# An audio tower on one core: scores and value products of two heads packed side by side in TensorE, a transposed group norm, and new start rounds

## Chip, cores and metric

The kernel runs on one core of a Trainium2 chip. Times are device microseconds (us) of one execution. Engines: PE is TensorE (PEld its weight loads), DVE is VectorE, ACT is ScalarE, POOL is GpSimd, SP is SyncE, which issues the DMAs.

## What is computed

The input is 32 sequences of 160,000 samples. Each is padded and cut into S = 313 frames of 512 samples. One layer of an audio tower follows (the reference, cut to what matters):

```python
h = frames @ dct.T                                   # (32, 313, 512)
X = layernorm(h)
Q, K = xpos(X W_Q), xpos(X W_K, downscale)           # 8 heads of 64
p = softmax(Q K^T) * gamma_h ** |s - t|
Y = groupnorm_per_head(p V) * gn_weight + gn_bias
h = h + (silu(X W_G) * Y) @ W_O
x = layernorm(h)
theta = x[..., None, :] / (1 + |W|) + B_param        # 256 units x 512 features
sin, cos = table(round(theta * 4096 / 2 pi) mod 4096)
h = h + silu(sum_d(cos * a_cos) @ P_cos.T + sum_d(sin * a_sin) @ P_sin.T)
```

The feature part is the large one: for each of 32 x 313 frames, 256 x 512 sines and as many cosines.

## The kernel before

The work has two kinds, which run interleaved on the same engines: **attention** of one sequence (function attention, L302), and **feature rounds** (ffn_round, from L574).

*Feature rounds.* The sequences go in 16 pairs. STARTS (L33) gives the round in which each pair enters; it stays eight rounds, one for each block of 32 of the 256 units. A round therefore works on one to four pairs, r = 2 to 8 sequences. A round has 128 (unit, 128 features) parts, taken in slots of up to 24 sequences x 313 columns. In each slot DVE computes indices, one instruction per part (L612), adds a quarter turn (L621) and masks (L628); ACT takes two sines of up to 7512 columns (L636), into one of two trig buffers; PE contracts them with a one-hot attention matrix into four-way column groups (L658). At the end of a round sums are copied (L675) and stored (L682, L688). The features of the ring come from DRAM (xT, L596), and the contraction's weights too (hot, L604).

*Attention.* A sequence uses one set of buffers, A: PSUM banks W (four), and in SBUF h (rows), u, xnT, prob (8 heads x 3 row tiles x 313). The rows are held in three tiles of N = 105 rows. In order: DCT (rows, L282), layer norm with Newton steps on POOL, transposes (L269), values (L282), rotated queries and keys for pairs of heads (columns, L297, then L360 and L363), scores, exponentials on ACT (L400), and for each head nine transposes of the probabilities (L428), the decay (L440), and the product with the values. Then the gate, the group norm, the output product, and the second layer norm, whose transposed result goes to xT_d (L525). A function output (L528) ends a pair once its eight rounds are over. The first two sequences run before any feature round, side by side, in buffers A and B; all others run in A beside the rounds. While one pair is in the ring (r = 2), attention takes its copies and row sums on ACT, otherwise on DVE.

*Steps that the change touches.* scores (L367): per head, three matmuls of 64 contracted rows x 313 columns into banks 0 to 2 (L374), then one maximum (L382) and one subtraction (L385) over 3 x 313 columns; the next head uses the same banks. Product with values (L446): for each head and row tile, three matmuls with the probabilities as weights and 64 columns of values, result in rows, copied for two heads at a time (L460). Group norm: square (L481 or L478), sum over 64 columns (L486), reciprocal and three small steps (L488 to L491), Newton on POOL, a POOL product (L495), a broadcast product (L498), twelve transposes (L269), weight and bias from PSUM (L509), product with the gate (L514).

*What sets the order.* Plan (L46) collects every step with a key, an engine, an expected duration and what it reads and writes. emit (L63) then simulates the engines and writes out, for each, the ready step with the smallest key. The keys of a feature round count sines: one unit is one full sine. attention spreads its keys over the time that it was given: step(n) adds n to a counter, and the key is that share of 135. The time for each sequence comes from STARTS: the kernel takes the tightest spacing that has each pair ready eight units before its round. What comes out is a fixed order on every engine; at run time an instruction also waits for the one ahead of it on its engine.

Of the kernel before, what the change touches and what calls it, by code (L numbers as in the profile page):

```python
# [21 lines left out]
P = 128  # L22
# [5 lines left out]
EPS = 1e-5  # L28
RING = 8
# [3 lines left out]
STARTS = (0, 4, 8, 10, 12, 14, 16, 18, 20, 22, 24, 26, 28, 30, 32, 34)  # L33
# [93 lines left out]
def tile_audio_tower(ctx: ExitStack, tc: tile.TileContext, t: dict, out: bass.AP):  # L127
# [23 lines left out]
    class Buffers:  # L151


        def __init__(self, name, pool, psum):
# [16 lines left out]
            self.h = sb("h", NT, HOP)  # L171
            self.xnT = sb("xnT", NC4, S)
# [11 lines left out]
            self.sq = wide[:, : NT * HOP].rearrange("p (i d) -> p i d", d=HOP)  # L184
            self.hres = self.sq
            self.aff = wide[:, NT * HOP : NT * HOP + NC4 * S].rearrange("p (c s) -> p c s", s=S)
            self.mx = [sb(f"mx{i}", NT) for i in range(2)]
# [7 lines left out]

            self.y = self.W[:, 3, : NT * 2 * DH].rearrange("p (i d) -> p i d", d=2 * DH)
# [24 lines left out]
    def rsqrt(plan, key, val, r, u, kv, kr, ku):  # L221
# [17 lines left out]
        plan.add(key, "POOL", 6000, newton, (kv,), (kr, ku))  # L239
# [24 lines left out]
    def transposed(plan, key, x):  # L264

        for c in range(NC4):
            def go(c=c):
                for i in range(NT):
                    nc.tensor.transpose(  # L269
                        x.W[:, c, ROW0[i] : ROW0[i] + N], x.h[:N, i, c * P : (c + 1) * P],  # L270
                        ident[:N, :N],
                    )
            plan.add(key, "PE", 800, go, x.rows_of, x.banks(c))

    def rows(plan, key, x, lhsT, src, r, order=range(NT), src_r=()):

        for c in range(NC4):
            k = x.load(plan, key, src[c], src_r)
            for to, i in enumerate(order):
                plan.add(  # L280
                    key, "PE", 880,
# [7 lines left out]
    def columns(plan, key, x, bank, src):  # L289
# [4 lines left out]
        for c in range(NC4):  # L294
            plan.add(
                key, "PE", 550,
# [5 lines left out]
    def attention(plan, keys, sq, x, eng, swap_m=None):  # L302
# [6 lines left out]
        def step(n=1.0):  # L309
            done[0] += n  # L310
            return keys(done[0] / 135.0)
# [14 lines left out]
        plan.add(step(0), "SP", DMA_NS, lambda: nc.sync.dma_start(x.u, t["frames"][sq]), (), us)  # L326
        rows(plan, step(7), x, x.u, t["dct"], us)
        copy(plan, step(), eng, NT * HOP, x.h[:N], W3, x.banks(0, 1, 2), hs)
        residual(step(0), False)
        layernorm(plan, step(3), x)  # L330
        transposed(plan, step(3), x)
        copy(plan, step(), eng, NC4 * S, x.xnT, x.W[:, :, :S], x.banks(0, 1, 2, 3), (x.k("xnT"),))


        rows(plan, step(7), x, x.xnT, wv_d, (x.k("xnT"),), range(NT - 1, -1, -1),
             ("wv_d",))
        copy(plan, step(), eng, NT * HOP, x.h[:N], W3, x.banks(0, 1, 2), hs)
        plan.add(step(0), "POOL", 500, lambda: nc.gpsimd.memset(x.h[0:1, : NT - 1, :], 0.0), (), hs)

        plan.add(step(0), "SP", DMA_NS, lambda: nc.sync.dma_start(x.table, t["turn_qk"]),  # L340
                 (), probs[-4:-2])

        def rotary(g):
            key = step(4)
# [7 lines left out]
            else:  # L352
                copy(plan, key, eng, 2 * S, x.raw, x.W[:, 0:2, :S], x.banks(0, 1), probs[-1:])
                for i in range(2):
                    plan.add(key, "PE", 550,
# [11 lines left out]
        def scores(hd):  # L367
            key = step(2.5)
            r0 = (hd % 2) * DH
            qk, kq = x.qk[hd // 2 % 2], x.k("u", hd // 2 % 2)  # L370
            for i in range(NT):
                plan.add(
                    key, "PE", 660,
                    lambda i=i: nc.tensor.matmul(  # L374
                        x.W[:N, i, :S], qk[r0 : r0 + DH, 0, ROW0[i] : ROW0[i] + N],
                        qk[r0 : r0 + DH, 1, :], start=True, stop=True,
                    ),
                    (kq,), x.banks(i),
                )
            m = x.mx[hd % 2]  # L380
            plan.add(key, "DVE", 1150,
                     lambda: nc.vector.tensor_reduce(m[:N], x.W[:N, :NT, :S], AX.X, ALU.max),  # L382
                     x.banks(0, 1, 2), (x.k("mx", hd % 2),))
            plan.add(key, "DVE", 1150,
                     lambda: nc.vector.tensor_tensor(  # L385
# [554 lines left out]
```

## Time and profile before

| what | us |
|---|---|
| median of 3 runs | 18587.15 (18586.4 to 18591.35) |
| the profiled execution's own time | 18593.15 |
| its span, first to last instruction | 18591.2 |
| ACT busy | 17827.2 |
| DVE busy | 17165.7 |
| PE busy | 14520.5 |
| POOL busy | 968.9 |

The span is 2 us shorter than the execution's own time. Busy times are of the profiled execution. In the groups a line reads: source line, engine, operation, output <- input, shapes, count | busy us, mean ns of one | idle us of the engine just before them, and what ended it. In the table of stages each row is a stretch of the span with each engine's busy us and its count of instructions, then PE's granted clock, the DMA share and GB/s. In the waits a row is the waiting engine and line, what it waited for, total us, times, longest us. An fp32 matmul leaves two records in the trace, a transpose one. A matmul's mean duration includes the time that it overlaps others, so PE's cost is taken as busy us divided by the count.

### The profile page before, as it was taken

The page shows a single profiled execution, that of the slowest core. Times are in us where ns is not written, and L with a number is a line of the kernel's source. Part 1 is how long each engine was busy: PE and PEld are TensorE (multiplying, and loading weights), DVE is VectorE, ACT ScalarE, POOL GpSimd, SP SyncE. Part 2 cuts the span into 40 slices and gives each one's busy share as a digit, 9 for nine tenths or more (in the row PEclk, how much of TensorE's full clock was granted, in tenths as well). Part 3 has the DMA queues.
Part 4 walks back from the last instruction along what each step waited for, and adds up shares of the span by engine and source line. Part 5 has one row for each costly group of instructions (what it writes and reads, how often), then busy time and mean ns, then how long its engine had stood idle before and what let it go on. Part 6 is the DMA issues. An engine that isn't in the chain of part 4 may idle for free. (4 is left out here: it accounts for less than half of the span.)

```text
span 18591.2 us, 325962 instructions
## 1 busy us (share of the span) xinstructions
PE 14520.5 (78%) x148768; PEld 6791.6 (37%) x148768; DVE 17165.7 (92%) x11210; ACT 17827.2 (96%) x3248; POOL 968.9 (5%) x1222
## 2 busy tenths in 40 slices
PE   8788888888777877778877787877788777666666
PEld 5443333334333333333333333333333333222222
DVE  6989999999999999999999999999999999888887
ACT  4899999999999999999999999999999999999998
POOL 0000000000000000000000000000000000000000
PEclk8899999999999999999999999999999999888888
DMA  3221121121111111111111111111111111001011
GB/s 94 71 66 56 60 67 58 54 61 58 45 38 47 57 50 52 45 45 57 48 58 47 43 53 48 58 48 55 39 50 57 48 56 42 29 21 33 20 40 53
DMA packets 598691, 942.55 MB, mean 51 GB/s; under 512 B 116768, under 2 KB 337952, under 8 KB 586048
## 3 DMA queue, kind: packets, MB, share of 16 engines
q1 hardware_dynamic: 597312, 921.70, 16.0%
q8 instruction: 1166, 19.10, 0.4%
q14 instruction: 213, 1.74, 0.0%
HBM read 816.78 MB, written 104.66 MB: 50 GB/s over the span
## 5 line engine op out<-in xcount | busy, mean ns | idle before, releaser
L636 ACT ACTIVATE trig<-ix 128x7512 f32<-128x7512 int16 (+1 forms) x2760 | 17398.1, 6386 | 456.8 <-PE pa L658 229.7
L658 PE MATMUL pa<-trig,hot 128*32 128x313 f32 x131072 | 10304.5, 468 | 3545.1 <-ACT trig L636 3530.3
L658 PEld LDWEIGHTS pa<-trig,hot 128*32 128x32 f32 x131072 | 4291.2, 118 | 9312.4 <-ACT trig L636 4578.4
L612 DVE TENSOR_SCALAR ix<-xT,f 128x2504 int16<-128x2504 f32 (+3 forms) x5376 | 6499.2, 1268 | 431.6 <-ACT trig L636 389.4
L628 DVE TENSOR_SCALAR ix<-ix 128x15024 int16<-128x15024 int16 (+4 forms) x1656 | 5581.8, 3385 | 41.1
L621 DVE TENSOR_SCALAR ix<-ix 128x7512 int16<-128x7512 int16 (+1 forms) x1380 | 2905.2, 2105 | 356.1 <-ACT trig L636 264.4
L297 PE MATMUL a_W<-a_xnT,a_ring 128*128 128x313 f32 x4896 | 1426.2, 437 | 40.9 <-DVE a_prob L385 15.4
L282 PE MATMUL a_W<-a_ring,a_u 128*105 128x512 f32 x2256 | 1087.5, 625 | 141.2 <-DMA a_u<-in_frames 52.9
L297 PEld LDWEIGHTS a_W<-a_xnT,a_ring 128*128 128x128 f32 x4896 | 891.8, 190 | 580.1 <-issue 212.5
L282 PEld LDWEIGHTS a_W<-a_ring,a_u 128*105 128x105 f32 x2256 | 374.7, 177 | 756.3 <-issue 615.0
L233 POOL TENSOR_TENSOR a_gu<-a_gr 105x24 f32<-105x24 f32 x93 | 104.5, 1124 | 9461.6 <-DVE a_gr L227 9456.7
L446 PE MATMUL a_W<-a_h,a_prob 105*105 105x64 f32 x4464 | 483.0, 264 | 77.6 <-DVE a_prob L440 77.4
L374 PE MATMUL a_W<-a_u 64*105 64x313 f32 x1488 | 477.7, 453 | 72.1 <-DVE a_prob L385 40.0
L446 PEld LDWEIGHTS a_W<-a_h,a_prob 105*105 105x105 f32 x4464 | 447.3, 177 | 212.1 <-issue 143.7
L282 PE MATMUL a_W<-a_ring,a_xnT 128*105 128x512 f32 x744 | 350.6, 611 | 22.3 <-DVE a_xnT L219 20.5
L233 POOL TENSOR_TENSOR a_lu<-a_lr 105x3 f32<-105x3 f32 x186 | 141.1, 759 | 4073.3 <-DVE a_lr L227 4063.6
L374 PEld LDWEIGHTS a_W<-a_u 64*105 64x105 f32 x1488 | 234.0, 171 | 310.8 <-DVE a_prob L385 79.2
L428 PE MATMUL a_W<-ident,a_prob 105*105 105x105 f32 x2232 | 284.9, 272 | 44.1 <-DVE a_h L460 26.1
L382 DVE TENSOR_REDUCE a_mx<-a_W 105x3 f32<-105x939 f32 x248 | 280.1, 1130 | 37.6 <-PE a_W L374 36.5
L428 PEld LDWEIGHTS a_W<-ident,a_prob 105*105 105x105 f32 x2232 | 237.9, 178 | 159.4 <-issue 92.5
L440 DVE TENSOR_TENSOR a_prob<-a_W,a_u 105x939 f32<-105x939 f32 x248 | 279.8, 1128 | 16.3 <-PE a_W L428 10.9
L385 DVE TENSOR_TENSOR a_prob<-a_W,a_mx 105x939 f32<-105x939 f32 x248 | 281.7, 1136 | 8.5
(134 smaller groups left out, 3386.8 us busy)
## 6 DMA issues: line engine op xcount, KB each, us to landing
hot<-in_hot SPq DMA_DIRECT2D x1344, 128.0 KB
xT<-xT_d SPq DMA_DIRECT2D x88, 1252.0 KB
a_u<-in_decay SPq DMA_DIRECT2D x248, 260.5 KB
a_ring<-in_proj SPq DMA_DIRECT2D x128, 256.0 KB
a_ring<-in_dct SPq DMA_DIRECT2D x124, 256.0 KB
a_ring<-wv_d SPq DMA_DIRECT2D x124, 256.0 KB
a_ring<-in_wq SPq DMA_DIRECT2D x124, 256.0 KB
a_ring<-in_wk SPq DMA_DIRECT2D x124, 256.0 KB
```

The source lines that it names most:

```text
L282: lambda c=c, i=i, k=k, to=to: nc.tensor.matmul(x.W[:N, to, :], lhsT[:, c, ROW0[i] : ROW0[i] + N], x.ring[k], start=(c == 0), stop=(c == N ...
L297: lambda c=c: nc.tensor.matmul(x.W[:, bank, :S], w[:, c, :], x.xnT[:, c, :], start=(c == 0), stop=(c == NC4 - 1)),
L374: lambda i=i: nc.tensor.matmul(x.W[:N, i, :S], qk[r0 : r0 + DH, 0, ROW0[i] : ROW0[i] + N], qk[r0 : r0 + DH, 1, :], start=True, stop=True,),
L382: lambda: nc.vector.tensor_reduce(m[:N], x.W[:N, :NT, :S], AX.X, ALU.max),
L385: lambda: nc.vector.tensor_tensor(x.prob[:N, hd], x.W[:N, :NT, :S], m[:N].unsqueeze(2).to_broadcast((N, NT, S)), ALU.subtract),
L428: nc.tensor.transpose(x.W[:N, jj, ROW0[i] : ROW0[i] + N], x.prob[:N, a, i, ROW0[j] : ROW0[j] + N], ident[:N, :N],)
L446: nc.tensor.matmul(x.y[:N, i, (hd % 2) * DH : (hd % 2 + 1) * DH], x.prob[:N, a, jj, ROW0[i] : ROW0[i] + N], x.h[:N, jj, hd * DH : (hd + 1) ...
L612: nc.vector.tensor_scalar(ix[:, x[0], pt * r * S : (pt + 1) * r * S], now["xT", y][:, : r * S], f[:, 0, n : n + 1], f[:, 1, n : n + 1], AL ...
L621: nc.vector.tensor_scalar(ix[:, x[1], :E], ix[:, x[0], :E], float(LUT // 4), None, ALU.add)
L628: nc.vector.tensor_scalar(ix[:, i, :E], ix[:, i, :E], LUT - 1, LUT // 2, ALU.bitwise_and, ALU.bitwise_xor)
L636: nc.scalar.activation(tl[:, :E], ix[:, x[1 - k], :E], AF.Sin, bias=-PI32, scale=ANG)
L658: nc.tensor.matmul(now["pa", p][g * 32 : g * 32 + 32, :S], now["hot", hot[n // 4 * 4, c]][:, n % 4, k, :], now["trig", w][:, s0 : s0 + S], ...
```

## The change

It has five parts.

1. *Planned durations and shares.* The key of attention's steps now follows a table of shares (SHARE, TIMES) instead of counts out of 135; several expected durations are changed. The feature matmuls' key becomes one unit smaller.
2. *Scores.* Two heads at a time: for each row tile one matmul of rows 0 to 63 and one of rows 64 to 127, into two banks; the next row tile takes the other two banks. Maximum and subtraction are taken for two heads x one row tile.
3. *Product with values.* For two heads, 3 x 2 matmuls with the values as weights (64 columns each, into PSUM rows 0 to 63 and 64 to 127) and 313 columns of probabilities. The result is transposed, two heads in one bank, and is copied so (yT). The values are kept in an order (v) that gives each pair of heads a stretch of its own, in the same buffer.
4. *Group norm in transposed form.* Square of yT; sums of each head by twelve matmuls with a 0/1 table of 8 columns; variance in two fused steps, which take the softmax's row sum in without a reciprocal; Newton as before; three transposes of the factors, a copy, four matmuls that spread them over the 512 features with gn_weight in the table; one product; bias and gate in one fused step for each of four tiles. The twelve transposes, the POOL product and the scaled copies go. Two small tables are loaded for each sequence.
5. *Start rounds.* STARTS is changed; there are 43 rounds where there were 42.

```diff
-STARTS = (0, 4, 8, 10, 12, 14, 16, 18, 20, 22, 24, 26, 28, 30, 32, 34)
+STARTS = (0, 4, 7, 9, 11, 13, 15, 17, 19, 21, 23, 25, 27, 29, 32, 35)
...
+SHARE = dict(rows=5.0, copy=2.5, norm=8.0, turn=0.7, rotary=4.2, scores=6.4, exps=2.0, head=3.5,
+             pair=0.8, gate=4.1, silu=1.5, group=7.0, affine=5.0)
...
-        def step(n=1.0):
-            done[0] += n
-            return keys(done[0] / 135.0)
+        def step(stage=None):
+
+            if stage:
+                done[0] += SHARE[stage]
+            return keys(done[0] / WHOLE)
...
+        def scores(g):
...
             for i in range(NT):
+                b = (g * NT + i) % 2 * 2
+                m, km = x.mx[(g * NT + i) % 2], x.k("mx", (g * NT + i) % 2)
+
+                def go(i=i, b=b):
+                    for a in range(2):
+                        nc.tensor.matmul(
+                            x.W[:N, b + a, :S], qk[a * DH : a * DH + DH, 0, ROW0[i] : ROW0[i] + N],
+                            qk[a * DH : a * DH + DH, 1, :], start=True, stop=True)
+                plan.add(key, "PE", 690, go, (kq,), x.banks(b, b + 1))
...
+            def go(g=hd // 2):
+                for jj in range(NT):
+                    for b in range(2):
+                        nc.tensor.matmul(
+                            x.W[b * DH : (b + 1) * DH, 3, :S],
+                            x.v[:N, jj, g, b * DH : (b + 1) * DH],
+                            x.prob[:N, 2 * g + b, jj, :], start=(jj == 0), stop=(jj == NT - 1))
+            plan.add(key, "PE", 1900, go, (*probs[hd - 1 : hd + 1], hs[hd // 2]), x.banks(3))
...
+        def sums():
+            for i in range(NT):
+                for c in range(NC4):
+                    nc.tensor.matmul(x.W[:N, 0, i * H : (i + 1) * H],
+                                     x.sqT[:, c, ROW0[i] : ROW0[i] + N], x.of_head[:, c, :],
+                                     start=(c == 0), stop=(c == NC4 - 1))
+        plan.add(key, "PE", 2400, sums, room, x.banks(0))
...
+            nc.vector.scalar_tensor_tensor(f(x.gv), f(x.sm), EPS, f(x.sm), ALU.mult, ALU.mult)
+            nc.vector.scalar_tensor_tensor(
+                f(x.gv), x.W[:N, 0, : NT * H], 1.0 / DH, f(x.gv), ALU.mult, ALU.add)
...
+        def factors():
+            for i in range(NT):
+                nc.tensor.transpose(x.W[:H, 1, ROW0[i] : ROW0[i] + N], x.gr[:N, i, :], ident[:N, :N])
...
+        def spread():
+            for c in range(NC4):
+                nc.tensor.matmul(x.W[:, c, :S], x.head_w[:, c, :], x.rT, start=True, stop=True)
...
+                     lambda: nc.vector.tensor_tensor(x.sqT, x.yT, x.W[:, :, :S], ALU.mult),
...
+                     lambda c=c: nc.vector.scalar_tensor_tensor(
+                         x.u[:, c, :], x.sqT[:, c, :], gnb[:, c : c + 1], x.u[:, c, :],
+                         ALU.add, ALU.mult),
...
-                plan.add(key, "PE", 150 * len(parts) * r, go,
+                plan.add(key - 1, "PE", 150 * len(parts) * r, go,
```

## The prediction

> **What bounds the kernel now.** I read the busy shares first, then the groups with the idle time before them, then the busy time by stage, and last who waited for whom.
>
> ```profile
> PE 14520.5 (78%) x148768; PEld 6791.6 (37%) x148768; DVE 17165.7 (92%) x11210; ACT 17827.2 (96%) x3248; POOL 968.9 (5%) x1222
> ...
> L636 ACT ACTIVATE trig<-ix 128x7512 f32<-128x7512 int16 (+1 forms) x2760 | 17398.1, 6386 | 456.8 <-PE pa L658 229.7
> L658 PE MATMUL pa<-trig,hot 128*32 128x313 f32 x131072 | 10304.5, 468 | 3545.1 <-ACT trig L636 3530.3
> ...
> L446 PE MATMUL a_W<-a_h,a_prob 105*105 105x64 f32 x4464 | 483.0, 264 | 77.6 <-DVE a_prob L440 77.4
> ...
> L374 PE MATMUL a_W<-a_u 64*105 64x313 f32 x1488 | 477.7, 453 | 72.1 <-DVE a_prob L385 40.0
> ```
>
> The sines (L636) are 17,398 of ACT's 17,827 us, and ACT's work is the same in both kernels. So the time is 17,827 us plus ACT's idle time, 18591.2 - 17827.2 = 764 us; a change can gain only from that. Where it lies, by stage (columns: start and end, length, then busy us of PE, weight load, DVE, ACT, POOL):
>
> ```profile
> 0.00:316.20 316.20, 265.07 (x992) 171.67 (x992) 144.94 (x178) 51.44 (x125) 19.96 (x82) 0.79 0.35 106
> 316.20:1003.00 686.80, 552.00 (x5104) 283.40 (x5104) 630.16 (x749) 587.07 (x201) 44.68 (x76) 0.89 0.24 72
> 1003.00:2215.00 1212.00, 985.73 (x9777) 483.37 (x9770) 1162.63 (x943) 1136.17 (x246) 69.68 (x89) 0.92 0.19 59
> 2215.00:2806.00 591.00, 481.71 (x4733) 224.76 (x4735) 569.60 (x468) 552.32 (x97) 42.91 (x63) 0.93 0.23 70
> 2806.00:4531.00 1725.00, 1413.30 (x14272) 686.80 (x14264) 1668.17 (x1128) 1663.91 (x281) 125.14 (x152) 0.94 0.18 57
> 4531.00:15750.00 11219.00, 8950.55 (x92936) 4185.94 (x92940) 10587.96 (x6210) 11079.16 (x1857) 666.55 (x760) 0.93 0.16 49
> 15750.00:18541.00 2791.00, 1845.53 (x20928) 746.51 (x20916) 2398.21 (x1536) 2754.23 (x445) 0.00 (x0) 0.88 0.10 32
> 18541.00:18591.20 50.20, 26.61 (x52) 9.17 (x48) 4.00 (x3) 2.90 (x2) 0.00 (x0) 0.77 0.34 97
> ```
>
> Length less ACT gives the idle time: **265 us** before the first sine, 100 + 76 + 39 + 61 = **275 us** in the ramp to 4531, **140 us** in the steady stage, **37 us** at the end, **47 us** after the last sine. In the first stage PE is the busy engine (265 of 316 us). In the ramp DVE is (92 to 97%). In the steady stage ACT itself is at 98.8%.
>
> ```profile
> ACT trig L636 <- PE pa L658: 229.7, 132, 8.8
> ACT trig L636 <- DVE ix L628: 128.1, 56, 13.4
> ACT trig L636 <- issue: 81.3, 21, 7.4
> ```
>
> These waits are the sines': for PE to give a trig buffer back, and for DVE to deliver indices. "issue" has no named cause; those that I followed in the timeline lay beside a held-up PE, and I count it with PE.
>
> [...] four 32-wide groups make one feature record cost 10304.5/131072 = 79 ns, against 1426.2/4896 = 291 ns for a full-width one of the same 313 columns (L297). For row halves no run shows it: L374 uses one half at a time, 477.7/1488 = 321 ns. [...] the trace's clock is 0.50 from 150 to 200 us, where the prelude does transposes and 64-column products.
>
> **The change, part by part.** An fp32 matmul leaves two records here, a transpose one.
>
> *PE, per sequence.* Removed: product of weights and values 483.0/31 = 15.6 us, scores 477.7/31 = 15.4, the gate's twelve transposes 1.7; in all 32.7. Added: 24 products of 313 columns, 48 x 291 ns = 14.0, halved when the two heads share the columns, 7.0; scores halved, 7.7; 12 sums at L446's 108 ns x 24 = 2.6; three transposes 0.4; four spreads 8 x 291 ns = 2.3. In all 20, so -12.7 us (if nothing overlaps: 34.7, +2). After the prelude PE is not the bound, so this alone counts little there.
>
> *DVE, per sequence.* Maxima and subtractions: 8 x (1130+1136) = 18.1 us become 24 x 809 = 19.4 (+1.3). Reduce, reciprocal and three small steps, 2.58, become two small ones, 0.37 (-2.2). L509 and L514, 3.85, become four of about 0.53 (-1.7). Square, product and result copies shrink with 1536 to 1252 columns and 0.55 to 0.48 us (-0.9). The copy of the factors adds 0.5. Sum **-3.0 us**. The fused operation and the one that reads PSUM are not in the trace; at 0.48 to 0.80 us each it is -3.2 to -1.9.
>
> *Starts of the pairs.* DVE's index instructions are 128 in every round however many sequences it holds; the four rows (602, 927, 1254, 1578 ns for 626 to 2504 columns) give a fixed 276 ns, so a round costs 35 us of DVE beyond its elements. The new starts have 43 rounds for 42, but reach the same point (the start of the sixth pair) in 13 rounds where it took 14. So the ramp loses 35 us of DVE work, and 70 us appear at the end, where DVE is at 86%. Sines: 2758 for 2760, no difference.
>
> *Prelude (265).* Two sequences run on PE. The heads' stage is 157.7 to 233.5 us, of blocks such as these:
>
> ```profile
> 213.38 3.38 PE L446 MATMUL a_W<-a_h,a_prob 105*105 105x64 f32 x18
> 216.56 1.86 PE L428 MATMUL b_W<-ident,b_prob 105*105 105x105 f32 x9
> ```
>
> Sixteen products at about 3.0 us are 48 us. They become eight of 12 records; [...] 2.7 us each: 22 us. That is -26 if paired, -4 if not. The scores took 47.7 us in two stretches, where PE and DVE took turns on the same banks; with alternating banks DVE alone sets them, 24 x 1.62 + 3 = 42: -5. The longer chain of the group norm (sums, factors, spread: three more PE hops and a copy) adds about 6 where PE has nothing else. **-25**, from -5 to -35.
>
> *Ramp (275).* DVE-paced, so DVE work removed comes back as time: 35 us and ten sequences by 3 us, -65. One stall is plain:
>
> ```profile
> 1005.30 1.77 DVE L612 TENSOR_SCALAR ix<-xT,f 128x1252 int16<-128x1252 f32 x2 [19.41 <-DMA xT<-xT_d]
> ```
>
> The second pair's features landed late, and ACT lost 13.4 us. In the order of the kernel as built, the last copy of that pair stood one slot (two sines) ahead of its round; it now stands 2.5 ahead, and at the later starts 2 to 9, where it was mostly 1 to 3. That is -13. The feature matmuls get a key one unit earlier, so attention goes before them only when it lags a sine; of the ramp's some 170 us of PE waits most will be overtaken by DVE, I take -17. **-95**, from -30 (only part of the DVE work) to -200 (DVE's floor is 4031 - 65 = 3966 us for 4215).
>
> *Steady (140).* 67 us of the waits here are PE's and 48 "issue". The earlier key and 12.7 us less PE work per sequence shorten the stretches for which a feature block stands behind attention; stalls in which PE waits for a transfer (L282 for in_frames, 34 us in 15 waits) stay. I take half of 115: **-60**, from 0 to -105.
>
> *End (84).* A third round of one pair costs DVE 143 us against ACT's 138, +5; the last output is as before. **+5**, from 0 to +20. The two table loads per sequence add two SP issues, each of 0.3 to 0.6 us like its neighbours, with the gate's columns to hide them; without that cover, under 1 us per sequence. The extra round brings 32 loads of hot, four of xT and four of f on SP, spread over 138 us. POOL loses one step (L495) and clears the same 1024 elements in four pieces; at 5% busy nobody waits for it.
>
> Sum -25 - 95 - 60 + 5 = **-175 us**. The profiled execution took 18593.15 us, 6 above the median of 18587.15, so against the median: **18,412 us** (-0.94%).
>
> **Rivals.** (a) *Pairs don't overlap in the array.* For it: row halves are in no trace[...]. Against: the column groups do overlap. The prelude keeps -5 and the steady stage loses a third: about 18,455. (b) *PE waits only change their name:* DVE has 94% in the steady stage and more in the ramp, so the freed sines wait for indices. Then -25, -50, -10, +5: 18,507. (c) *The stalls nearly all go*, since accurate durations let the written order fit the chip: -30, -170, -100, 0: 18,290. (d) *Slower: attention falls behind.* One buffer serves every sequence in turn; three more PE hops now stand behind feature blocks of 3.4 us each, and the spacing in the ramp shrinks from 64 to 58.7 sines (413 to 379 us). If the last copy comes later than about two slots before its round, each start costs ACT the 13.4 us seen above; at all 15 starts 201 us, more than the gain from the fourteenth start on: 18,613. Against: the order as built has the copies earlier, not later. (e) The change does what it says: the built kernel has the counts above, so this is not open.
>
> **How the numbers follow.** Main case 0.55 (18,340 to 18,470), (a) 0.12, (b) 0.18, (c) 0.10, (d) 0.05. The range 18,300 to 18,515 covers the main case, (a), (b) and part of the way to (c). About 0.2%, 37 us, is what a measurement of this kernel can tell from no change: faster needs under 18,550. From the cases: faster 0.92, same 0.05, slower 0.03.
>
> **What would show it.** First sine near 290 us for 316; 12-record products near 2.7 us in the prelude; scores' groups at about 160 ns of PE a record; DVE busy about 60 us lower (-97 + 35); ACT busy within 5 us of 17,827; PE waits of the sines near half of 230; no wait of 19 us for xT at the fifth round. It is wrong if ACT's idle time in the ramp stays above 240 us, or if the sines' waits for DVE grow by what those for PE lose.

## The result, and the profile after

The changed kernel takes **18551.99 us** (median of 20 runs, 18542.69 to 18563.74) against 18588.39 for the kernel before (20 runs): a ratio of **0.9981, with an interval from 0.9975 to 0.9987**. It is faster by 36 us where 175 were predicted, and it lies above the range. The profiled execution has a span of 18548.7 us, 42.5 less than before.

The page of the changed kernel, busy times and then the groups that the change was about (line, engine, operation, shapes, count | busy us, mean ns | idle us before them):

```profile
PE 14237.3 (77%) x146432; PEld 6376.6 (34%) x146432; DVE 17101.3 (92%) x11500; ACT 17818.3 (96%) x3246; POOL 1062.2 (6%) x1190
...
L660 ACT ACTIVATE trig<-ix 128x7512 f32<-128x7512 int16 (+1 forms) x2758 | 17391.4, 6391 | 430.3 <-PE pa L682 184.7
L682 PE MATMUL pa<-trig,hot 128*32 128x313 f32 x131072 | 10303.9, 468 | 3675.0 <-ACT trig L660 3636.7
...
L391 PE MATMUL a_W<-a_u 64*105 64x313 f32 x1488 | 267.5, 465 | 123.3 <-DVE a_mx L396 103.1
...
L466 PE MATMUL a_W<-a_prob,a_h 105*64 105x313 f32 x1488 | 235.0, 452 | 41.2 <-DVE a_prob L455 40.8
```

The work went the way that was forecast, on PE with less of it gone. The scores (L391) are 267.5/1488 = 180 ns a record for 321 before (160 forecast), the products of values and weights (L466) 235.0/1488 = 158 ns for the 291 of a full-width record, so in both the two of a pair run together. PE has 283 us less, 9 per sequence where 12.7 were forecast; DVE has 64 us less (62 forecast). The maxima and subtractions of 626 columns, forecast at 809 ns, took 801 and 809 (L396, L400); before, an operation on two tensors of that width took 811 (L363). The fused steps of 313 columns, forecast at 0.53 us, took 0.54 (L535). But the sines' idle time fell only from 456.8 to 430.3 us.

Stage by stage, as before, but cut where the same sine starts (sine 0, 610 and 2340, counted from 0, each cut within 0.3 us; columns: start and end, length, busy us of PE, weight load, DVE, ACT, POOL, then clock, DMA share and GB/s). First the kernel before, then the changed one:

```profile
0.00:316.50 316.50, 265.07 (x992) 171.67 (x992) 145.24 (x179) 51.74 (x125) 19.96 (x82) 0.79 0.35 106
316.50:4568.30 4251.80, 3465.83 (x34147) 1691.55 (x34148) 4059.62 (x3312) 3965.81 (x827) 290.49 (x392) 0.92 0.20 62
4568.30:15862.30 11294.00, 9002.35 (x93488) 4206.44 (x93486) 10648.62 (x6231) 11158.63 (x1871) 658.47 (x748) 0.93 0.16 50
15862.30:18591.20 2728.90, 1787.24 (x20144) 721.95 (x20144) 2312.18 (x1492) 2651.02 (x429) 0.00 (x0) 0.87 0.10 31
```

```profile
0.00:313.60 313.60, 227.86 (x846) 122.09 (x846) 138.31 (x190) 51.21 (x125) 17.91 (x80) 0.83 0.36 108
313.60:4534.20 4220.60, 3383.19 (x33496) 1570.55 (x33496) 4018.18 (x3228) 3975.82 (x827) 353.46 (x370) 0.92 0.21 61
4534.20:15830.50 11296.30, 8801.53 (x91692) 3928.07 (x91692) 10557.84 (x6318) 11147.77 (x1865) 669.49 (x716) 0.93 0.17 49
15830.50:18548.70 2718.20, 1824.73 (x20400) 755.91 (x20398) 2386.98 (x1766) 2643.48 (x433) 21.38 (x24) 0.89 0.13 38
```

So the difference in length is **-2.9 in the prelude, -31.2 in the ramp, +2.3 in the steady stage and -10.7 at the end**, where -25, -95, -60 and +5 were forecast. The forecast was of ACT's idle time, which is length less ACT's busy time: 264.8 and 262.4 us, 286.0 and 244.8, 135.4 and 148.5, 77.9 and 74.7, so **-2, -41, +13 and -3**. The two counts differ because the same number of sines is not the same work: some sines, those of the last slot of a round, have fewer than 7512 columns. Counted in full sines of 7512 columns, the ramp holds 599.3 before and 601.3 after, and the end 414.7 and 412.0.

The steady stage gained nothing although PE has 201 us less to do in it (9002.4 to 8801.5) and DVE 91. Its waits, of the sines and then of PE (PE's own waits for sines left out):

```profile
ACT trig L660 <- issue: 107.0, 25, 7.5
ACT trig L660 <- PE pa L682: 35.0, 19, 4.7
```

```profile
PE a_W L391 <- DVE a_mx L396: 68.7, 41, 3.4
PE a_W L517 <- POOL a_gr L247: 60.0, 18, 5.0
```

Before, those two rows of the sines had 48.5 and 62.2 us. The wait for PE was halved, as forecast, and the one without a named cause doubled. PE's second row is new: the factors' transposes (L517) stand for POOL's Newton steps. One such place in the timeline (POOL, PE, DVE and ACT mixed, weight loads left out; start us, length us, then in brackets the idle time ahead and its releaser):

```profile
9979.29 4.07 DVE L652 TENSOR_SCALAR ix<-ix 128x15024 int16<-128x15024 int16 x1
9979.44 3.99 POOL L246 TENSOR_SCALAR a_gu<-a_gu 105x24 f32<-105x24 f32 x1
9980.58 3.37 PE L682 MATMUL pa<-trig,hot 128*32 128x313 f32 x48 [1.45 <-ACT trig L660]
...
9988.07 0.21 POOL L246 TENSOR_SCALAR a_gu<-a_gu 105x24 f32<-105x24 f32 x1
9988.36 0.23 POOL L247 TENSOR_TENSOR a_gr<-a_gr,a_gu 105x24 f32<-105x24 f32 x1
9988.65 0.69 PE L517 MATMUL a_W<-ident,a_gr 105*8 105x105 f32 x3 [4.70 <-POOL a_gr L247]
9989.38 0.47 DVE L520 COPY a_prob<-a_W 8x313 f32<-8x313 f32 x1 [3.02 <-PE a_W L517]
...
9989.90 4.54 PE L524 MATMUL a_W<-a_prob 8*128 8x313 f32 x8 [0.57 <-DVE a_prob L520]
...
9994.37 8.23 PE L682 MATMUL pa<-trig,hot 128*32 128x313 f32 x96
...
9999.56 12.82 ACT L660 ACTIVATE trig<-ix 128x7512 f32<-128x7512 int16 x2 [6.33 <-issue]
```

Read it from the bottom. ACT lost 6.33 us at 9999.56. It needed a trig buffer that PE gives back with a feature block, and PE's last block had ended at 9983.95. Until 9994.37, for 10.4 us, PE did none: it stood 4.70 us for POOL, transposed, waited for a copy, and spread the factors. A feature block frees one buffer and takes 3.4 us; a sine takes 6.4. The POOL step L246 took 3.99 us here, where it lay beside DVE's L652 and ended 0.07 us after it, and 0.21 us at 9988.07. The whole Newton chain took 13.0 us here; the planner was told 7.5.

Part of the 10.4 us is a slower PE. In the table of stages, cut at this place, the granted clock stands third from the right (a block ahead of the wait, the wait, the stretch behind it, the next block):

```profile
9980.58:9983.95 3.37, 3.37 (x48) 1.46 (x48) 3.37 (x2) 3.37 (x1) 3.29 (x2) 1.00 0.00 0
9983.95:9988.65 4.70, 0.00 (x1) 0.00 (x1) 2.40 (x2) 4.70 (x2) 3.99 (x9) 0.89 0.09 28
9988.65:9994.37 5.72, 5.15 (x11) 2.70 (x12) 4.08 (x3) 4.58 (x1) 0.00 (x0) 0.50 0.01 3
9994.37:9999.56 5.19, 5.19 (x57) 2.13 (x60) 5.05 (x6) 0.00 (x0) 0.00 (x0) 0.66 0.39 121
```

The clock was 1.00 in the first 3.5 us of the stand and 0.50 from 4 us on, and 0.50 through the stretch behind it. The eight records of the spread (L524) took 4.54 us; at 4936.49 us, at a clock of 1.00, they took 2.37. ACT got its buffer 5.2 us after the block behind them began, where a block at a clock of 1.00 took 3.37 (at 9980.58). An estimate from these figures: about 4 of the 6.33 us that ACT lost came with the slower clock (4.54 - 2.37 and 5.2 - 3.37), the rest with the stretch itself. Of the 19 such places of the steady stage the spread took over 4.5 us in 13.

### The profile page after: what moved, and what is told of

It is laid out like the page before. It is cut to its first block, busy times and chain, and to the rows that moved or that the text cites. A ratio compares the mean times of both kernels' runs of the same rounds, so it can differ in the third digit from the quotient of the medians.

```text
span 18548.7 us, 322240 instructions
## 1 busy us (share of the span) xinstructions
PE 14237.3 (77%) x146432; PEld 6376.6 (34%) x146432; DVE 17101.3 (92%) x11500; ACT 17818.3 (96%) x3246; POOL 1062.2 (6%) x1190
## 5 line engine op out<-in xcount | busy, mean ns | idle before, releaser
L660 ACT ACTIVATE trig<-ix 128x7512 f32<-128x7512 int16 (+1 forms) x2758 | 17391.4, 6391 | 430.3 <-PE pa L682 184.7
L636 DVE TENSOR_SCALAR ix<-xT,f 128x2504 int16<-128x2504 f32 (+3 forms) x5504 | 6535.1, 1246 | 145.8 <-ACT trig L660 111.2
L652 DVE TENSOR_SCALAR ix<-ix 128x15024 int16<-128x15024 int16 (+4 forms) x1655 | 5582.3, 3387 | 43.0
L308 PE MATMUL a_W<-a_xnT,a_ring 128*128 128x313 f32 x4896 | 1452.9, 440 | 34.3 <-DVE a_prob L374 8.9
L244 POOL TENSOR_TENSOR a_lu<-a_lr 105x3 f32<-105x3 f32 x186 | 186.0, 1000 | 4411.5 <-DVE a_lr L238 4239.7
L400 DVE TENSOR_TENSOR a_prob<-a_W,a_mx 105x626 f32<-105x626 f32 x372 | 301.1, 809 | 76.9 <-PE a_W L391 58.8
L391 PE MATMUL a_W<-a_u 64*105 64x313 f32 x1488 | 267.5, 465 | 123.3 <-DVE a_mx L396 103.1
L396 DVE TENSOR_REDUCE a_mx<-a_W 105x2 f32<-105x626 f32 x372 | 297.9, 801 | 26.3 <-PE a_W L391 20.5
L466 PE MATMUL a_W<-a_prob,a_h 105*64 105x313 f32 x1488 | 235.0, 452 | 41.2 <-DVE a_prob L455 40.8
L374 DVE TENSOR_TENSOR a_prob<-a_W,a_prob 128x1252 f32<-128x1252 f32 x124 | 180.6, 1457 | 45.6 <-PE a_W L370 37.7
L428 DVE TENSOR_REDUCE a_sm<-a_prob 105x6 f32<-105x1878 f32 x108 | 220.0, 2100 | 0.0
```

Source lines behind the costliest of these rows:

```text
L244: nc.gpsimd.tensor_tensor(u, r, r, ALU.mult)
L308: lambda c=c: nc.tensor.matmul(x.W[:, bank, :S], w[:, c, :], x.xnT[:, c, :], start=(c == 0), stop=(c == NC4 - 1)),
L396: lambda b=b, m=m: nc.vector.tensor_reduce(m[:N], x.W[:N, b : b + 2, :S], AX.X, ALU.max),
L400: lambda i=i, b=b, m=m: nc.vector.tensor_tensor(x.prob[:N, 2 * g : 2 * g + 2, i, :], x.W[:N, b : b + 2, :S], m[:N].unsqueeze(2).to_broadca ...
L636: nc.vector.tensor_scalar(ix[:, x[0], pt * r * S : (pt + 1) * r * S], now["xT", y][:, : r * S], f[:, 0, n : n + 1], f[:, 1, n : n + 1], AL ...
L652: nc.vector.tensor_scalar(ix[:, i, :E], ix[:, i, :E], LUT - 1, LUT // 2, ALU.bitwise_and, ALU.bitwise_xor)
```

## The experiments

Theory: the steady stage's gain went into this new stretch of PE. Rivals: PE's total of attention work between blocks holds the sines whatever its order; or the earlier key or the new starts did the harm. All changes are against the changed kernel unless said otherwise. Stages are cut at the same sines, from one profiled execution each; the medians are of all runs of each kernel. The kernel before was run again beside each group of experiments, with medians from 18585.8 to 18595.1 us, and the ratios are to those; a difference of 10 us between two experiments is within that spread.

| kernel | median us | to sine 0 | to 610 | to 2340 | to the end |
|---|---|---|---|---|---|
| before | 18588.4 | 316.5 | 4251.8 | 11294.0 | 2728.9 |
| changed | 18552.0 | 313.6 | 4220.6 | 11296.3 | 2718.2 |
| 1 Newton planned at 16 us | 18474.9 | 312.8 | 4214.3 | 11229.1 | 2716.9 |
| 2 Newton on DVE | 18456.8 | 313.0 | 4218.9 | 11207.3 | 2717.1 |
| 3 key back | 18558.5 | 318.2 | 4228.2 | 11286.4 | 2711.8 |
| 4 starts back | 18574.2 | 319.9 | 4222.3 | 11320.7 | 2724.0 |
| 5 order in the prelude | 18541.1 | 310.8 | 4223.1 | 11290.7 | 2716.7 |
| 6 scores back | 18538.9 | 311.9 | 4226.6 | 11292.6 | 2717.2 |
| 7 all Newton on DVE | 18508.5 | 307.4 | 4252.9 | 11223.1 | 2720.4 |
| 8 = 2 + 5 | 18450.7 | 311.1 | 4206.4 | 11210.6 | 2717.0 |
| 9 spread one block later | 18444.9 | 318.4 | 4213.2 | 11193.4 | 2714.0 |
| 10 = 2 + 4 | 18474.0 | 314.7 | 4218.1 | 11209.8 | 2724.0 |
| 11 = 2 + 5 + 6 | 18448.0 | 306.0 | 4209.8 | 11220.8 | 2710.5 |
| 12 = 11, prelude's Newton on DVE | 18431.1 | 300.3 | 4205.2 | 11222.0 | 2714.1 |
| 13 = 9 + 5, prelude's Newton on DVE | 18438.5 | 309.1 | 4217.4 | 11203.6 | 2713.1 |
| 14 = 13 + 6 | 18413.8 | 302.0 | 4219.7 | 11177.2 | 2714.0 |
| 15 norm ahead of the gate | 18428.3 | 308.8 | 4185.1 | 11215.7 | 2713.7 |
| 16 = 14 + 15 | 18403.8 | 293.2 | 4217.2 | 11178.2 | 2708.1 |

Kernels with the same order on PE up to the first sine (the changed one, 2, 3 and 4 among them) put it anywhere from 313.0 to 319.9 us, so first sines are compared below by their pieces.

**1, a longer planned duration of Newton.**

```diff
-        plan.add(key, "POOL", 7500, newton, (kv,), (kr, ku))
+        plan.add(key, "POOL", pool, newton, (kv,), (kr, ku))
...
-        rsqrt(plan, key, x.gv[:N], x.gr[:N], x.gu[:N], x.k("gv"), x.k("gr"), x.k("gu"))
+        rsqrt(plan, key, x.gv[:N], x.gr[:N], x.gu[:N], x.k("gv"), x.k("gr"), x.k("gu"),
+              16000 if eng == "DVE" else 7500)
```

> The changed kernel (18552 us) with one number different: the planner takes 16 us, not 7.5, for POOL's Newton steps of the group norm (as they take 12.6 to 13 us in the steady stage of the trace), which puts three feature blocks instead of two between the sums and the factors' transposes on PE, and in most sequences one more block before the spread. My theory, that PE standing for POOL in those transposes (60 us in 18 waits of the steady stage) is where the steady stage lost what it was to gain: the wait falls below 10 us, the sines' idle time without a named cause (107 us in the steady stage) halves, and the time falls by 40 to 70 us, to about 18,500. Rival, that the sines are held by PE's total of attention work between blocks and the wait only changes its name: within 15 us of 18,552.

18474.89 us, ratio to before 0.9941 (0.9929 to 0.9954), 77 us below the changed kernel. The sines' wait without a cause fell to 41.3 us, but PE's wait for POOL only to 40.7. The expected size of the gain was right and its reason only half: PE still waits, and yet the sines hardly do.

**2, the group norm's Newton on DVE.**

```diff
+        e = nc.vector if on == "DVE" else nc.gpsimd
...
-                nc.gpsimd.tensor_tensor(u, r, r, ALU.mult)
+                e.tensor_tensor(u, r, r, ALU.mult)
```

> The changed kernel with the group norm's Newton steps on DVE instead of POOL in all sequences but the first three pairs' single ones; the same arithmetic, 12 small instructions of about 0.17 us, 2 us of DVE per sequence. My theory: the hand-off to POOL and back is gone, PE's wait in the factors' transposes falls from 60 us to under 15, and the time falls by 30 to 60 us, a little less than with the longer planned duration because DVE gets 2 us per sequence. Rival, that DVE's share (92%) decides: no better than 18,552, or up to 30 us slower by 28 sequences times 2 us less the waits.

18456.83 us (0.9931, 0.9918 to 0.9945). This step on DVE took 182 to 185 ns in all its 81 places:

```profile
L247 DVE TENSOR_TENSOR a_gu<-a_gu,a_gv x81: 182/183/185, 1682.4 to 16158.1; 105x24 f32<-105x24 f32 x81
```

so twelve are 2.2 us of DVE for 13 us of POOL. The steady stage gained 89 us, more than expected; DVE's larger share did not decide.

**9, only the spread moved.** In 1 the planner had also put a feature block between the factors' transposes and the spread. So this was done alone:

```diff
-        plan.add(step(), "DVE", 500,
+        plan.add(step(), "DVE", 3000 if eng == "DVE" else 500,
                  lambda: nc.vector.tensor_copy(x.rT, x.W[:H, 1, :S]), x.banks(1), (room[1],))
```

> The changed kernel with one number different: the planner takes 3 us, not 0.5, for the copy of the factors, which puts one feature block on PE between the factors' transposes and the spread; POOL's Newton steps and the two blocks ahead of the transposes stay. Theory A, that the sines stop because wait, transposes, copy and spread make one stretch of PE of some 10.5 us without a feature block: PE still stands for POOL (about 60 us in the steady stage), but the sines' idle time without a named cause falls from 107 us to 40 to 60, and the time by 40 to 70 us. Theory B, that PE's wait for POOL is itself lost to the sines: within 15 us of 18,552.

18444.93 us (0.9924, 0.9911 to 0.9936): 107 us from one number in a planner's table. The steady stage's waits, of the sines and of PE, and one of its places:

```profile
ACT trig L660 <- PE pa L682: 31.6, 19, 4.2
ACT trig L660 <- issue: 7.6, 4, 3.5
```

```profile
PE a_W L517 <- POOL a_gr L247: 48.5, 18, 4.8
```

```profile
9943.42 0.43 PE L517 MATMUL a_W<-ident,a_gr 105*8 105x105 f32 x3 [1.39 <-POOL a_gr L247]
9943.79 3.37 PE L682 MATMUL pa<-trig,hot 128*32 128x313 f32 x48
...
9947.08 2.37 PE L524 MATMUL a_W<-a_prob 8*128 8x313 f32 x8
9949.38 3.37 PE L682 MATMUL pa<-trig,hot 128*32 128x313 f32 x48
```

PE still waits 18 times for POOL, 48.5 us for 60.0, and the sines' unexplained idle time is gone, 107.0 to 7.6. The wait of the place shown is short; but where PE stood 4.77 us (at 7713.21), and the block behind the transposes took 4.53 us for 3.37, the sines lost 0.75 us. So theory A holds and B falls: **most of what is lost is not the wait but the length of PE's stretch between two feature blocks**. PE has the slack for one wait of up to 4.8 us (at most 2.4 us are lost behind one), not for a wait, a copy and a spread in a row.

The clock is part of this: in the changed kernel it was 0.50 in the spreads of 4.54 us and 1.00 in those of 2.37. In 9 all 19 spreads of the steady stage take 2.37 us, and in 2, where PE has no wait for POOL, 17 of 19 do. In 9 a feature block lies between PE's wait and the spread. No run holds the clock and lengthens the stretch, so how the gain divides between the two is not shown.

**7, all Newton steps on DVE**, those of the layer norms too (the twelve instructions of `newton` on `nc.vector`, planned at 2200).

> The changed kernel with all Newton steps on DVE, those of the layer norms too; 12 small instructions each, about 2.2 us on DVE by the second experiment's trace (0.18 us each). Theory, that DVE loses as much by standing for POOL in the layer norm (48.7 us in 35 waits in the steady stage, 27.3 in 18 in the ramp) as the steps cost it, while the chain of each sequence gets shorter by some 20 us: within 15 us of the second experiment's 18,457, and in the prelude, where Newton on POOL took 3.4 us and the chain is bare, the first sine some 5 us earlier. Rival, DVE's work decides: 62 layer norms times 2.0 us less 90 us of waits, 20 to 60 us slower than 18,457.

18508.52 us: the rival was right. Beside experiment 2 the ramp is 34 us longer, with 4078.7 us of DVE work in it for 4033.2, and the steady stage 16. The ramp does follow DVE's work, at 34 us of time for 46 of work.

**3, the key of the feature matmuls put back** (`key - 1` to `key`).

> The changed kernel with the feature matmuls' key put back (no unit earlier), everything else as changed. If the earlier key gave part of the gain, as the prediction had it (some 17 us in the ramp and part of 60 in the steady stage): 30 to 60 us slower than 18,552. If the earlier key did nothing, or only pushed the attention behind feature blocks: within 15 us, or faster.

18558.52 us, 6 more than the changed kernel: within the measurement. The earlier key was worth nothing that shows.

**4, the old starts**, and **10, the old starts with Newton on DVE.**

```diff
-STARTS = (0, 4, 7, 9, 11, 13, 15, 17, 19, 21, 23, 25, 27, 29, 32, 35)
+STARTS = (0, 4, 8, 10, 12, 14, 16, 18, 20, 22, 24, 26, 28, 30, 32, 34)
```

> The changed kernel with the starts of the pairs as before (0, 4, 8, 10, ... 34). If the new starts gave what the prediction had them give (35 us of DVE in the ramp, 13 us for the stall at the second pair, less 5 at the end): 30 to 45 us slower, about 18,590, with the 13 us stall of the sines at the fifth round back. If the ramp is not paced by DVE's work: within 15 us.

> The group norm's Newton steps on DVE, with the starts of the kernel before. The fourth experiment gave the new starts some 22 us, of which 24 lay in the steady stage, where two more sequences stood in the wait for POOL. If the starts' gain was only that: within 8 us of the second experiment's 18,457. If the starts save time of their own: 18,475 to 18,490.

18574.21 us for the first (0.9995 of before, 0.9987 to 1.0004: without the new starts the changed kernel is not measurably faster than the one before) and 18473.96 for the second. So the new starts are worth 22 us in the changed kernel and 17 without the wait for POOL, between the two expectations. The ramp is as long with the old starts (4222.3 for 4220.6; 4218.1 for 4218.9), but less is done in it: by sine 610 ACT has 12 us fewer of sines behind it (599.3 full sines for 601.3). In ACT's idle time the ramp has 258.7 us in 4 for 244.8, and 255.1 in 10 for 242.9 in 2. So 12 to 14 us of the gain lie in the ramp, where 35 were forecast. In 4 the steady stage is 24 us longer too, with 20 of the POOL waits for 18 (its profiled execution, 18588.6 us, is one of its slower ones); in 10 that is gone. The end is 6 to 7 us longer with the old starts because more sines are left for it (414.7 full ones for 412.0); ACT's idle time there is the same within 1 us. The stall of 13 us at the second pair, which experiment 4 should have brought back, did not come: no row with xT is among its DVE waits of the ramp. The attention's new plan had removed it, not the starts.

**5, the order in the prelude.** PE took the third sequence's first products before the second sequence's last transposes, and waited for their frames.

```diff
-        rows(plan, step("rows"), x, x.u, t["dct"], us)
+        rows(plan, step("rows"), x, x.u, t["dct"], (*us, ("xT_d", 1)) if sq == 2 else us)
```

> The changed kernel with one line more for the planner: the third sequence's first products count as following the second sequence's result, so PE takes them after the second sequence's last transposes and not before (in the trace PE stood 8.9 us for the third sequence's frames and 4.4 us in the product, with those transposes behind it). My theory, that this put back what the shorter heads' stage of the prelude had gained: first sine 10 to 13 us earlier than at 313.4, near 302 us, and the whole 5 to 13 us faster than 18,552. Rival, that the second sequence's own chain is not ready earlier: first sine within 2 us of 313.4, the whole within 10 us.

18541.06 us. From the second sequence's addition (L541) to the first sine it took 34.3 us for 41.9, a gain of 7.6 where 10 to 13 were expected; the first sine came only 2.8 us earlier, since this execution was 4.7 us later at the addition. **8** put it together with 2:

> The group norm's Newton steps on DVE together with the third sequence's first products behind the second sequence's result. If the two causes add up: 18,457 less 5 to 13 us, about 18,448. If the order in the prelude gives nothing: 18,457.

18450.71 us, 6 less than 2; so it adds, at the size of a measurement's spread.

**6, the scores of the kernel before**: one head at a time into banks 0 to 2, maximum and subtraction of 939 columns (the old `scores`, `mx` of three columns).

> The changed kernel with the scores of the kernel before: one head at a time, three products into banks 0 to 2, one maximum and one subtraction of 939 columns. All other parts as changed. Theory from the trace, that in the prelude alternating banks gave nothing, because the maximum, the subtraction and the next product of the same sequence follow each other by hand-offs (about 56 us of scores in the changed kernel against 47.7 in the one before): first sine some 8 us earlier than 313.4. In the rest DVE loses 1.3 us less per sequence and PE takes 7.7 us more per sequence: within 25 us of 18,552 either way. Rival, the prediction's: the side by side scores are worth 5 us in the prelude, so the first sine comes 5 us later, and PE's 7.7 us more per sequence cost the steady stage 20 to 60 us.

18538.86 us, 13 less than the changed kernel (ratio 0.9976, 0.9967 to 0.9985, which overlaps the changed kernel's interval). The last exponential of the prelude came at 167.3 us for 174.7, as the trace had suggested; 5 of these 7 us were given back in the heads' stage, 44.1 for 39.1 us. Side by side, many of the steps look like this, with PE at a clock of 0.50:

```profile
101.50 0.80 DVE L396 TENSOR_REDUCE b_mx<-b_W 105x2 f32<-105x626 f32 x1
102.36 1.38 PE L391 MATMUL b_W<-b_u 64*105 64x313 f32 x4 [1.63 <-DVE b_mx L396]
103.78 0.81 DVE L400 TENSOR_TENSOR b_prob<-b_W,b_mx 105x626 f32<-105x626 f32 x1 [1.48 <-PE b_W L391]
```

DVE stands 1.48 us for a product of 1.38 that started only once the maximum before it had been taken: the products and the maxima take turns after all. In the steady stage the old scores changed nothing (11292.6 for 11296.3), though such scores took PE 15.4 us per sequence in the kernel before (477.7/31) and the paired ones 8.6 (267.5/31).

**15, the first half of the group norm ahead of the gate** (squares, sums, variance and Newton are written before the gate's `columns` and silu; nothing else).

> The changed kernel with the first half of the group norm (squares, sums, variance, Newton steps) written ahead of the gate's products instead of after them, so that the sums use their bank before the gate fills it; nothing else. Theory, that the group norm's longer chain in the prelude (10 us more from the last decay to the addition than before, where 6 were predicted) comes from the sums waiting for a bank that the gate holds until its silu: from the last decay to the addition 58 us become about 50, first sine 5 to 9 us earlier for the same start, and PE no longer stands for POOL in the factors' transposes, which gives the steady stage 50 to 100 us; in all 18,450 to 18,490. Rival, that the chain is long by its own hand-offs, wherever it stands: from decay to addition within 2 us of 58, first sine unchanged; only the wait for POOL goes.

18428.34 us (0.9911, 0.9896 to 0.9926). The sums use bank 0, which the gate fills. In the changed kernel they stood behind the gate's silu; here they come ahead of most of its products (changed kernel first, then experiment 15):

```profile
230.56 1.21 ACT L480 ACTIVATE b_u<-b_W 128x1252 f32<-128x1252 f32 x1 [9.48 <-PE b_W L308]
231.82 2.38 PE L501 MATMUL b_W<-b_prob 128*105 128x8 f32 x24 [1.30 <-ACT b_u L480]
```

```profile
222.74 1.25 ACT L484 ACTIVATE b_prob<-b_h 128x1252 f32<-128x1252 f32 x1 [11.32 <-DVE b_gv L499]
...
224.76 2.30 PE L492 MATMUL b_W<-b_prob 128*105 128x8 f32 x24
```

From the second sequence's last decay to its addition it took 48.2 us, where the changed kernel took 57.8 and the one before 47.5. So the chain was long by its place behind the gate, and the rival falls. PE itself stood only 1.30 us for the silu that held the bank; how much of the 9.6 us is the bank, and how much that the gate's products now run on PE while the norm's small steps are under way, this run does not separate. In the steady stage Newton now has the gate's products to hide behind, and no row of PE's waits names POOL any more.

**11 to 14 and 16, what helps, together.**

> Group norm's Newton steps on DVE, the third sequence's first products behind the second's result, and the scores of the kernel before (one head at a time). If the side by side scores cost what the sixth experiment suggests: 18,451 less up to 13 us. If with PE's waits gone PE's extra 7.7 us per sequence is felt: 10 to 40 us slower than 18,451.

> As the run before it, and in the first two sequences all Newton steps on DVE, those of the layer norms too, where the seventh experiment's first sine came 5.6 us earlier: 3 to 6 us faster than the run before it, first sine near 305 us. If that gain was the spread of the first sines between runs: the same.

> The longer planned copy of the ninth experiment, the third sequence's first products behind the second's result, and the first two sequences' Newton steps on DVE; POOL's steps elsewhere and the scores side by side as changed. If steady stage and prelude add: 18,445 less 10 to 13 us, 18,432 to 18,435, first sine near 305 us, and the 2340th sine some 11,195 us after the 610th.

> As the run before it, with the scores of the kernel before. If the old scores help only in the prelude (first sine 5 us earlier in the eleventh experiment) and not in the steady stage (where that experiment took 14 us longer than the second between the 610th and 2340th sine): within 10 us of the run before it, first sine near 300 us. If they help throughout: 10 to 20 us faster, about 18,418.

> The fourteenth run's kernel (18,414) with the group norm's first half ahead of the gate. If the bank was the cause and the gains add: first sine near 295 us for 302, about 18,405. If the earlier sums only lengthen PE's stretches elsewhere: no better than 18,414.

18448.00, 18431.13, 18438.50, 18413.75 and 18403.81 us. The old scores gave 3 us (8 to 11) and 25 (13 to 14), in the steady stage +10 and -26: better in all three comparisons, but 13 (in 6) and 3 us are within the spread, and their size in the steady stage is not settled. Experiment 12 gained 17 us where 3 to 6 were expected, 5.7 of them before the first sine; where the rest lies its profile does not show. Experiment 13 came 3 us above its expectation, and 16 met its own. The last kernel, ratio **0.9900 (0.9883 to 0.9916)**, is the fastest, with the first sine at 293.2 us.

## Why the prediction was wrong, point by point

**Steady stage, -60 forecast, +2 measured (+13 in ACT's idle time).** The step that failed is this one: "the earlier key and 12.7 us less PE work per sequence shorten the stretches for which a feature block stands behind attention". The work went (201 us of PE), and the wait for PE with a name fell from 62 to 35 us. But the new chain of the group norm made one longer stretch, once per sequence, and the idle time without a name rose from 48.5 to 107.0. The prediction had looked at POOL ("at 5% busy nobody waits for it") and at PE's added hops ("about 6 where PE has nothing else", in the prelude alone), but not at both together: the Newton steps' reader had been DVE (L498, 20.3 us of waiting in the ramp), which cost the sines little, and became PE. At the place shown PE's clock fell from 1.00 to 0.50 while PE stood for them, and the spread took 4.54 us for 2.37 and the block behind it 5.2 for 3.37. That the Newton chain is long could be read before: its twelve POOL steps take 10.3 to 13.0 us there in the steady stage, for 3.6 in the prelude. With the stretch broken up (9) the steady stage gains 101 us on the kernel before, so the forecast's direction was right and its 60 too little. The key, of which part of this was expected, gave nothing (3).

**Ramp, -95 forecast, -31 measured.** Three terms. "35 us and ten sequences by 3 us, -65": up to sine 610 DVE's work fell by 41 us. With the old starts (4) it fell by 33, close to the attention's 30, and the time by 30, but with the stall's 13 in it. Of the 35 us of the starts 12 to 14 came as time. The fixed cost of a round was saved: 1663 index instructions (L636) in the ramp for 1785 with the old starts. But DVE's total is only 9 us lower there, since by the same sine it had computed 15,024 more columns of indices, two slots; and ACT had done 12 us more of sines (3975.8 busy for 3963.6, of which attention is 136.0 in both). Why no more than 12 to 14 us came is not shown. "That is -13": the stall went, but DVE's idle time in the ramp rose from 192 to 202 us, since the new hand-offs (L520, L528 and L509, 23.7, 9.0 and 7.8 us) took the place of L498's 20.3 and of the stall's 19.4. "I take -17" for the key: nothing that shows (3). In ACT's idle time the ramp gave 41 of the 95.

**Prelude, -25 forecast, -3 measured.** In pieces of the second sequence, before and after: to the last exponential 171.8 and 174.7 us; to the last decay 59.3 and 39.1; to the addition 47.5 and 57.8; to the first sine 37.6 and 41.8. The heads' stage gave 20 of its 26 us. Its two first paired blocks of 12 records took 3.40 us at a clock of 0.50, where 2.7 were forecast, the author's estimate: it was too little, since the 291 ns of a full-width record at a clock of 0.93 make some 0.54 us at 0.50, an estimate, and 0.57 was measured for a pair of records. The other six took 1.8 us at a clock of 1.00; over that stage it was 0.87 (174.7 to 213.8 us) and not 0.59 as before (157.7 to 233.5), which the prediction did not foresee. "-5" for the scores was +3 (6: PE and DVE take turns on each bank pair). "About 6" for the chain of the group norm was 10 (15: its place behind the gate, whose bank it shares). The order at the end (5) cost 7.6, of which 4.2 are new. With all of it mended (16) the first sine is at 293.2, 23 us earlier: the gain was there, and was given back three times.

**End, +5 forecast, -11 measured.** The end holds 2.7 full sines fewer, 17 us, and 10 us more of attention on ACT. In ACT's idle time it is -3. DVE's 75 us more (70 forecast) did not show as time.

The signs that the prediction named: PE's pairing (180 ns for about 160), DVE's busy time and the missing stall at the fifth round came true; the first sine, the blocks of 12 records, ACT's busy time (17818, 9 less, where 5 were allowed), the sines' waits for PE (184.7 us for about 115) and the ramp's idle time (245 us, over the 240 named) did not. Of the rivals, (b), that PE's waits only change their name, is nearest, but it is not its mechanism: the freed sines did not wait for indices (in the steady stage that wait is 12.8 us before and 3.4 after, in the whole kernel 128.1 and 85.1).

What stays open: how the loss of a stretch divides between its length and PE's clock; why the new starts gave 12 to 14 of 35 us in the ramp; why the ramp is 35 us shorter in experiment 15 and not in 16, and the scores' effect in the steady stage.

## What to carry to other kernels

Where one engine feeds another in blocks from two buffers, ask of every step that is moved onto the feeding engine how long a stretch without a block it makes, with the waits inside it, and not how much work it is: one block put in the middle was worth 107 us, about three times what the whole change had gained. Look at the feeding engine's clock in the stretch too: here it was 0.50 in the spread behind each of the eleven stands of over 3 us. And when two kernels are compared stage by stage, cut at equal work, or compare the idle time of the engine that bounds them. When a result that a slow helper engine delivers gets a new reader, look up how long the helper really takes at that place and who stands behind the new reader. And check which bank a new step borrows: where it shares it with another step, its place in the order sets how long the chain is.

## What the runs showed of the hardware

A POOL step of 24 columns (L246) took 0.21 us at 9988.07 us, with no DVE step beside it, and 3.99 us at 9979.44, beside a DVE step on the indices (L652, 4.07 us), and ended 0.07 us after it; the longest such step (L247) took 4.05 us. What lengthens the POOL step no run shows. The same work on DVE took 183 ns a step (2).

Two row halves of the array in two banks ran together: 180 ns a record (L391) for 321 (L374 before). Two column halves: 158 ns (L466) for the 291 of a full-width record (L297 before).

PE's granted clock was 1.00 in the block ahead of a stand of 4.70 us, 0.50 in the 5.7 us behind it, and 0.66 in the next 5.2. In the steady stage of the changed kernel each of the eleven stands of over 3 us is followed by a spread of 4.5 us, and so are two of about 2 us; where PE has no such stand (2), 17 of 19 take 2.37. The clock was 0.50 in those of 4.5 us and 1.00 in those of 2.37 of the changed kernel. Whether it is the stand that lowers the clock is not shown: no run varied it alone.
